# A four-layer conv/attention kernel on one core: TensorE steps of the later layers issued one or two turns after their other parts

## Chip, core and metric

The kernel runs on one core of a Trainium2 chip. The metric is the device time of one execution in microseconds (us): a median of several runs, beside the lowest and the highest. A profile is one more execution, taken by the hardware profiler. Four engines compute: TensorE (PE; its weight loads are shown apart as PEld), VectorE (DVE), ScalarE (ACT) and GpSimd (POOL). SyncE (SP) issues the DMAs. Each engine takes its own instructions in the order in which the program lists them, and waits where an operand or a buffer isn't ready.

## What is computed

Sixteen images of 128 channels and 28x28 pixels pass through four layers. Everything is fp32 (`_gn`, `_ln_t`: group and layer norm).

```python
# layer 0: minus the L1 distance of every 3x3 patch to 128 filters
x = x + _L0_conv_ref(_gn(x), L0_conv_W)       # -sum_k |w[f,k] - patch[k]|
# layer 1: two 3x3 convs, weights and activations quantized to 4 bits
x = _L1_conv_ref(x, w1, w2, ...)
t = _to_tokens(x)                             # 784 tokens of 128 channels
# layer 2: scores[i,j] = sum_d v[d]*tanh(Wi[j,d] + Wi[i,d]); softmax; values
t = t + _L2_attn_ref(_ln_t(t), W, v)
t = t + _L2_ffn_ref(_ln_t(t), ...)            # 8 experts, the best 2 mixed
# layer 3: causal linear attention, then 16 spectral filters as convolutions
t = t + _L3_attn_ref(_ln_t(t), W, b)
t = t + _L3_ffn_ref(_ln_t(t), sigma, phi, M_u, M_phi_plus, M_phi_minus, ...)
```

## The kernel before

**Layer 0 sets the beat.** The images go through in five groups (`GROUPS`) of 2, 4, 4, 4 and 2 images. |w - x| is made as ACT's Abs (L1444, "a" tiles) or, by 2 max(w, x) - w - x, as DVE's max (L1446) and add (L1448, "m" tiles): one wide instruction for one filter and one tap or two. `sums` (L1457) then adds over the channels on PE, with a one-column selector (`sel`) as weights, 32 output rows at a time, so four matmuls run side by side in the array. One round of this is a *tick*: one tile for each list of filters. The groups have 528, 960, 864, 864 and 416 ticks. `taps_of` makes the tiles of tick k+2 (`AHEAD = 2`) while `sums` uses those of tick k; the tiles lie in slots of the buffer `work`, five of them for groups of four images, of which other parts may borrow one or two (`lend`). The sums of a *phase* (a quarter or a half of a group's filters) gather in two PSUM banks; two pairs of banks (`acc0` to `acc3`) take turns from phase to phase, and `tap_sums_out` empties a pair with two ACT instructions (L607) three ticks after its phase.

**Everything else is laid into the ticks.** Four `Lane`s hold generators that yield `EV` (a step for the other engines) or `PE` (a step for TensorE): `plain` (small sums for layer 0), `convs` (layer 1), `chain` (layers 2 and 3 but for scores and filters, image after image) and `conv_out` (the spectral filters). In each tick `ahead` runs the due EV steps of every lane, `sums` follows, then `behind` runs the PE steps of the lanes in the same tick. A rate for each lane, times a pace for the group, says how many steps are due. The attention scores are a fifth stream: 196 turns for each image, each four rows of tanh on ACT (L1021) and four score products on PE (L1005) into one PSUM bank `sp`, issued in the same tick; `rows` gives them out. After 28 turns the bank is multiplied by `near` into `sc` (L1032, L1034) and started anew (L1001). A turn that may not run yet is lost.

The steps that are named below: the chain's attention values (`av`, L1089), expert products (`ex` L1174 on PE, then four multiply-adds on DVE, L1178) and linear attention (`nu`, L1227 and L1244) all pass through one PSUM bank `psx`. `spectral` takes 64 jobs for each image: three matmuls with a band matrix (`u`, L1336, 392, 264 and 136 columns) into the one bank `psu`, an ACT copy (L1346), and a matmul of the copy into `out` (L1339). Band and matrix come by DMA two jobs ahead.

After the last tick comes the tail (`stage["alone"]`): scores, chain and filters that are left. There a turn of scores makes its arguments with four DVE adds (L1014) and one wide ACT tanh (L1016), and the freed `acc` banks join `psx` and `psu`.

PE's order is fixed as it was written (`in_traced_order`); the order of the other engines is arranged by a scheduler when the program is built.

Of the kernel before, what the change touches and what calls it, by code (L numbers as in the profile page):

```python
# [53 lines left out]
class Group:  # L54
# [7 lines left out]
    def __init__(self, first, n, plan, rows, pace):  # L62
        self.first, self.n, self.plan, self.rows, self.pace = first, n, plan, rows, pace
        self.tall = n * HW
# [15 lines left out]
def tiles(taps):  # L80
# [16 lines left out]
GROUPS = (Group(0, 2, ALONE, 0.0, 1.0), Group(2, 4, EARLY, 0.85, 0.9), Group(6, 4, BESIDE, 1.95, 1.0),  # L97
          Group(10, 4, BESIDE, 1.95, 1.0), Group(14, 2, LATE, 3.2, 1.6))
# [25 lines left out]
STEP = 208  # L124
RATE_X, RATE_Y, RATE_C, RATE_A, RATE_0, RATE_T, RATE_Z = 1.2, 0.93, 1.5, 1.5, 0.9, 2.0, 0.75
# [5 lines left out]
class Lane:  # L131

    def __init__(self, rate=1.0):
        self.gens, self.turn = [], None
        self.holds, self.others = False, ()
        self.rate, self.due = rate, 0.0
# [4 lines left out]
    def run(self, turn):  # L143


        while self.gens:
            if self.turn is None:
                self.turn = next(self.gens[0], None)
                if self.turn is None:
                    self.gens.pop(0)  # L150
            elif self.turn != turn or (turn == PE and any(o.holds for o in self.others)):
                return False
            else:
                self.turn = next(self.gens[0], None)
                self.holds = turn == PE
                if self.turn is None:
                    self.gens.pop(0)
                return True
        return False

    def tick(self, pace):
        self.due += self.rate * pace
        n = int(self.due)
        self.due -= n
        return n
# [49 lines left out]
def kernel(ctx: ExitStack, tc: tile.TileContext, a: dict, out: bass.AP):  # L215
# [4 lines left out]
    three = ctx.enter_context(tc.tile_pool(name="three", bufs=3))  # L220
    scratch = ctx.enter_context(tc.tile_pool(name="scratch", bufs=1, space=bass.MemoryType.DRAM))
# [8 lines left out]
    turns = {"psx": 0, "psu": 0, "row": 0, "th": 0}  # L230

    def bank(pool, tag, more, name):
        turns[tag] = (turns[tag] + 1) % (1 + len(more)) if stage["alone"] else 0
        if turns[tag]:
            pool, tag = psacc, more[turns[tag] - 1]
        return pool.tile([P, 512], F32, tag=tag, name=name)

    def ps(name):
        return bank(psx, "psx", ("acc0", "acc1"), name)

    def small(name):
        return bank(psu, "psu", ("acc2", "acc3"), name)
# [175 lines left out]
    nc.vector.tensor_copy(edge[:NB], q[:NB, : 2 * P])  # L418
    taken, which_in = {}, []
    for plan in PLANS:  # L420
        taken[plan.name] = const.tile([2 * NB, P], F32, name=f"taken_{plan.name}")
        nc.vector.memset(taken[plan.name], 0.0)
# [9 lines left out]
        nc.vector.tensor_tensor(taken[plan.name][:NB], which[:NB, :P], which[:NB, P:], ALU.add)  # L432
# [122 lines left out]
    def plain_taps(g, phase, accs):  # L555
# [22 lines left out]
        seen = seen_in.ap[: 2 * NB].rearrange("p (h w) -> p h w", w=HW)  # L578
# [21 lines left out]
    def tap_sums_out(g, phase, accs):  # L600

        s = take(1)
        if s is None:
            return False
        t = s.ap[:, :T]
        for c in range(2):
            nc.scalar.activation(t[:, c * NCK : (c + 1) * NCK], accs[c][:, :NCK], AF.Identity,  # L607
                                 bias=sw[g.plan.name][:, phase : phase + 1])
# [3 lines left out]
        return True  # L612
# [160 lines left out]
    def spectral_weights():  # L773
# [56 lines left out]
        for j in range(NAR):  # L830
            yield EV
            m = three.tile([P, P], F32, tag="mat", name=f"m_ar{j}")
# [3 lines left out]
        for k in range(NK):  # L836
            yield EV
            me = three.tile([P, P], F32, tag="mat", name=f"m_even{k}")
            mo = three.tile([P, P], F32, tag="mat", name=f"m_odd{k}")
# [110 lines left out]

    state, scored, attended, spectral_in, spectral_out = {}, set(), set(), {}, set()

    def head(b):
# [17 lines left out]
        while b and b - 1 not in scored:  # L971
            yield EV
        wi = one.tile([P, T + SPAN], F32, tag="wi", name=f"wi{b}")
# [7 lines left out]
        state[b] = t, mv, rstd, wi  # L981

    products = []

    sp = pss.tile([P, 512], F32, name="sp")
    nc.vector.memset(sp, 0.0)

    def scores(b):
# [6 lines left out]
        def products_of(m, rows):  # L995
# [12 lines left out]
        for ib in range(NT):  # L1008
            for m in range(Q):
# [13 lines left out]
                products.append(lambda m=m, rows=rows: products_of(m, rows))  # L1023
                yield
            while products:
                products.pop(0)()
            while ib == 0 and b and b - 1 not in attended:
                yield
            lo = ib * TB
            n = min(SPAN, T - lo)  # L1030
            dst = sc[:, ib, :]
            nc.vector.tensor_tensor(cols(dst, lo, n), in_rows(sp[:, :n]), in_rows(near[:, :n]), ALU.mult)  # L1032
            if n < SPAN:
                nc.vector.tensor_tensor(cols(dst, 0, SPAN - n), in_rows(sp[:, n:SPAN]), in_rows(near[:, n:]), ALU.mult)  # L1034
        scored.add(b)
# [232 lines left out]
    def spectral(b):  # L1268
# [10 lines left out]
        def fetch(n):  # L1279
            if n < len(jobs):  # L1280
# [3 lines left out]
                m = three.tile([P, P], F32, tag="mat", name=f"mat{b}_{n}")  # L1284
# [3 lines left out]
        for to in range(2):  # L1288
# [38 lines left out]
            for n in [*mine, None]:  # L1327
                yield PE
                if n is not None:
                    _, k, odd = jobs[n]  # L1330
                    fetch(n + 2)
# [5 lines left out]
                while len(copied) > (stage["alone"] and n is not None):  # L1337
                    u, m0, lag = copied.pop(0)
                    nc.tensor.matmul(acc[:, lag:TH], m0, u[:, : TH - lag], start=False, stop=n is None and not copied)  # L1339
                if n is not None:  # L1340
                    yield EV
                    if stage["alone"]:
                        u = row(TH)
                    else:
                        u = two.tile([P, TH], F32, tag="u", name=f"us{b}_{n}")
                    nc.scalar.copy(u[:, :TH], q[:, :TH])  # L1346
                    copied.append((u, m, odd and (to ^ odd)))
# [12 lines left out]
    first = Lane(RATE_X)  # L1360
# [4 lines left out]
    plain, convs, chain, conv_out = Lane(), Lane(RATE_C), Lane(RATE_X), Lane(RATE_Y)  # L1365
    lanes = plain, convs, conv_out, chain
    for lane in (plain, convs, conv_out):
        lane.others = [x for x in (plain, convs, conv_out) if x is not lane]
    chain.add(quantized_weights(), token_constants(), spectral_weights(), head(0))
# [18 lines left out]
    pace = {"by": 1.0, "rows": 1.0}  # L1388

    def rows(rate):  # L1390
        due["units"] += rate * pace["rows"]
# [4 lines left out]
    def ahead():  # L1396


        chain.rate = RATE_A if "attending" in state else RATE_X if stage["group"] else RATE_0
        ns = [lane.tick(pace["by"]) for lane in lanes]  # L1400
        for n, lane in zip(ns, lanes):
            for _ in range(n):
                lane.run(EV)
        return ns

    def behind(ns):
        for n, lane in zip(ns, lanes):
            for _ in range(n if lane is convs else n > 0):
                lane.run(PE)

    def whole(rate):

        rows(rate)
        ns = ahead()
        while products:
            products.pop(0)()
        behind(ns)
# [48 lines left out]
    outs = []  # L1466
    parity = 0
    for k, (i, phase, _) in enumerate(seq):
# [4 lines left out]
        if new_group:  # L1473
            stage["group"] = i
            length = sum(x[0] == i for x in seq)
            end = k + length
            pace["rows"] = STEP * g.n / 2 / length
# [76 lines left out]
```

## Time and profile before

| what | us |
|---|---|
| three runs, median (lowest to highest) | 11791.2 (11789.41 to 11796.64) |
| the profiled execution, its own time | 11793.19 |
| its span, first to last instruction | 11791.4 |
| layer 0's groups in the trace, by the normed inputs (L548) | 47, 847, 2808, 5552, 8287 to 10058 |
| tail | 10058 to 11791 |
| last score product | 11466 |

The span is the time between the first and the last instruction of the core, and the time of the execution is the span and some two microseconds around it. A *busy* share is the union of an engine's instructions over the span. PE's ends are modelled: a matmul of 392 columns is drawn some 495 ns long, while the next one starts after 330 ns, so short idle times of PE don't show. "Idle before" and the waits are time in which an engine had nothing running, put down to the instruction that released it. PEclk is the share of full clock that TensorE was granted.

### The profile page before, as it was taken

How to read it: one execution, taken by the hardware profiler on the slowest of the kernel's cores; microseconds unless marked ns; L12 is line 12 of the kernel's file. 1: busy time of each engine (PE TensorE's matmuls, PEld its weight loads, DVE VectorE, ACT ScalarE, POOL GpSimd, SP SyncE). 2: the span in 40 equal slices, each digit the busy share in tenths (PEclk: the TensorE clock that was granted, in tenths of full speed). 3: DMA queues.
4: the chain of work that ended last, by engine and by line, in shares of the span. 5: the costliest groups of instructions: out<-in, count | busy, mean ns of one | idle time of the engine just before them, and what ended most of it. 6: DMA issues, size and time to landing. Idle time of an engine off the chain costs nothing.

```text
span 11791.4 us, 237615 instructions
## 1 busy us (share of the span) xinstructions
PE 11008.6 (93%) x99720; PEld 4985.0 (42%) x99720; DVE 10167.6 (86%) x12868; ACT 9795.4 (83%) x13475; POOL 185.9 (2%) x142
## 2 busy tenths in 40 slices
PE   7998888899989989899999999989999999999999
PEld 3443333344434434344344443434444444444446
DVE  9998999888888888888888889888888888988882
ACT  7887999788789798897878979788787888888882
POOL 1000000000000000000000000000000000000000
PEclk9999999999999999999999999999999999999999
DMA  1210000001001101011011110101111111121113
GB/s 33 63 38 5 4 1 4 5 21 46 25 11 30 34 21 37 24 35 47 24 29 36 34 36 20 38 18 38 39 36 41 45 34 41 46 58 52 56 54 109
DMA packets 435153, 402.95 MB, mean 34 GB/s; under 512 B 63429, under 2 KB 418045, under 8 KB 433709
## 3 DMA queue, kind: packets, MB, share of 16 engines
q1 hardware_dynamic: 433650, 385.96, 11.6%
q8 instruction: 786, 12.88, 0.4%
q14 instruction: 285, 2.33, 0.1%
q10 hardware_dynamic: 432, 1.77, 0.0%
HBM read 363.03 MB, written 24.49 MB: 33 GB/s over the span
## 4 chain that ended last, share of the span: by engine, by line
PE 64%; DVE 25%; ACT 7%; issue 3%; POOL 0%; DMA 0%; SPq 0%; DVEq 0%; ACTq 0%; POOLq 0%
PE acc L1457 26%; PE sp L1005 12%; PE u L1336 11%; DVE work L1446 10%; DVE work L1448 8%; PE out L1339 5%; ACT rows_in L1021 4%; DVE work L1014 3%; PE conv_ps L645 3%; ACT work L1444 2%; PE ex L1174 2%; PE av L1089 1%; DVE t L1178 1%; DVE rows_in L1446 0%; ACT work L1016 0%
## 5 line engine op out<-in xcount | busy, mean ns | idle before, releaser
L1021 ACT ACTIVATE rows_in<-wi 128x394 f32<-128x394 f32 x9576 | 5126.0, 618 | 538.8 <-PE sp L1005 535.1
L1446 DVE TENSOR_SCALAR work<-work,w 128x3024 f32<-128x3024 f32 (+5 forms) x3050 | 4444.7, 1484 | 841.4 <-PE acc L1457 797.6
L1457 PE MATMUL acc<-work,sel_m 128*32 128x392 f32 (+3 forms) x39248 | 3905.2, 495 | 254.2 <-DVE work L1448 197.5
L1444 ACT ACTIVATE work<-work,w 128x2916 f32<-128x2916 f32 (+2 forms) x1242 | 2872.9, 2331 | 633.8 <-PE acc L1457 578.7
L1448 DVE SCALAR_TENSOR_TENSOR work<-work,w 128x2916 f32<-128x2916 f32 (+3 forms) x1154 | 3202.2, 2780 | 11.0
L1457 PEld LDWEIGHTS acc<-work,sel_m 128*32 128x32 f32 x39248 | 1257.2, 111 | 2223.7 <-issue 1677.0
L1005 PE MATMUL sp<-rows_in,vz 128*32 128x394 f32 x19152 | 2171.7, 499 | 13.5 <-ACT rows_in L1021 13.2
L1457 PE MATMUL acc<-work,sel_a 128*32 128x351 f32 (+2 forms) x16592 | 1742.4, 480 | 29.3 <-ACT work L1444 29.2
L1336 PE MATMUL u<-band,up 128*128 128x392 f32 (+2 forms) x6144 | 1629.9, 402 | 8.5 <-ACT y L650 3.9
L1336 PEld LDWEIGHTS u<-band,up 128*128 128x128 f32 x6144 | 1095.1, 190 | 953.4 <-issue 264.4
L1016 ACT ACTIVATE work<-work 128x1576 f32<-128x1576 f32 x742 | 1089.2, 1522 | 112.1 <-DVE work L1014 107.7
L1005 PEld LDWEIGHTS sp<-rows_in,vz 128*32 128x32 f32 x19152 | 700.2, 111 | 980.8 <-issue 655.2
L1014 DVE TENSOR_SCALAR work<-wi 128x394 f32<-128x394 f32 x2968 | 1039.1, 420 | 6.2 <-PE sp L1005 3.2
L1457 PEld LDWEIGHTS acc<-work,sel_a 128*32 128x32 f32 x16592 | 593.5, 111 | 773.2 <-issue 667.9
L1005 PE MATMUL sp<-work,vz 128*32 128x394 f32 x5936 | 591.7, 508 | 70.2 <-ACT work L1016 69.8
L1339 PE MATMUL out<-us,mat 128*128 128x392 f32 (+1 forms) x1366 | 563.0, 494 | 0.0
L1346 ACT COPY us<-u 128x392 f32<-128x392 f32 x683 | 322.1, 472 | 211.9 <-PE u L1336 211.0
L1178 DVE SCALAR_TENSOR_TENSOR t<-ex,gate,t 128x128 f32<-128x128 f32 x896 | 310.6, 348 | 141.9 <-PE ex L1174 129.2
L1346 ACT COPY rows_in<-u 128x392 f32<-128x392 f32 x341 | 164.5, 482 | 303.3 <-PE u L1336 302.0
L1174 PE MATMUL ex<-ew,xt 128*128 128x512 f32 x448 | 251.5, 645 | 106.0 <-DVE t L1178 96.2
L1005 PEld LDWEIGHTS sp<-work,vz 128*32 128x32 f32 x5936 | 148.8, 110 | 387.6 <-ACT work L1016 196.3
L1339 PE MATMUL out<-rows_in,mat 128*128 128x392 f32 (+1 forms) x682 | 280.1, 495 | 0.0
(319 smaller groups left out, 5707.0 us busy)
## 6 DMA issues: line engine op xcount, KB each, us to landing
band<-band SPq DMA_DIRECT2D x1024, 196.0 KB
mat<-mats SPq DMA_DIRECT2D x1024, 64.0 KB
lags<-lag_mats SPq DMA_DIRECT2D x80, 192.0 KB
work<-q_L_conv_w SPq DMA_DIRECT2D x16, 576.0 KB
ew<-in_L_ffn_expert_w_dram SPq DMA_DIRECT2D x16, 512.0 KB
work<-in_x_dram SPq DMA_DIRECT2D x10, 784.0 KB
eb<-eb_rows SPq DMA_DIRECT2D x16, 448.0 KB
band<-band_out SPq DMA_DIRECT2D x32, 196.0 KB
```

Source lines behind the costliest of these rows:

```text
L1005: nc.tensor.matmul(sp[32 * j : 32 * j + 32, lo : lo + WIN], vz[:, 32 - m : 64 - m], rows[j], start=m == 0, stop=m == Q - 1, skip_group_che ...
L1014: nc.vector.tensor_scalar(th[:, j, :], wi[:, i + Q * j : i + Q * j + WIN], wi[:, i + Q * j : i + Q * j + 1], None, ALU.add)
L1016: nc.scalar.activation(th, th, AF.Tanh)
L1021: nc.scalar.activation(rows[j], wi[:, i + Q * j : i + Q * j + WIN], AF.Tanh, bias=wi[:, i + Q * j : i + Q * j + 1])
L1174: nc.tensor.matmul(q, blk(xt, i), ew[:, 4 * h : 4 * h + 4, :], start=True, stop=True)
L1336: nc.tensor.matmul(q[:, P * i : TH], up[:, to ^ odd, i, :], t[:, :w], start=i == 0, stop=i == 2)
L1339: nc.tensor.matmul(acc[:, lag:TH], m0, u[:, : TH - lag], start=False, stop=n is None and not copied)
L1346: nc.scalar.copy(u[:, :TH], q[:, :TH])
L1444: nc.scalar.activation(part, x, AF.Abs, bias=wk, scale=-1.0)
L1446: nc.vector.tensor_scalar(part, x, wk, None, ALU.max)
L1448: nc.vector.scalar_tensor_tensor(part, x, wk, part, ALU.max, ALU.add)
L1457: nc.tensor.matmul(in_rows(accs[c][32 * j : 32 * j + 32, :NCK])[:, lo - 14 * c : hi - 14 * c, c0:c1], sel[kind][:, 31 - m : 63 - m], d.rea ...
```

## The change

The lanes get a rate for each group in steps a tick, and a lag: after a lane's EV step its next PE step may run only that many ticks later. In groups two to four the lags are 1 (plain, convs), 2 (conv_out) and 1 (chain); in the last group only conv_out has one, of 1; the first group and the tail have none. In each tick a lane runs at most one PE step. `hurry` drops the lag for the step that makes `wi`.

```diff
-GROUPS = (Group(0, 2, ALONE, 0.0, 1.0), Group(2, 4, EARLY, 0.85, 0.9), Group(6, 4, BESIDE, 1.95, 1.0),
-          Group(10, 4, BESIDE, 1.95, 1.0), Group(14, 2, LATE, 3.2, 1.6))
+BALANCED = (0.5, 0.75, 0.27, 0.75), (1, 1, 2, 1)
+GROUPS = (Group(0, 2, ALONE, 0.0, (0.4, 0.6, 0.35, 0.355), (0, 0, 0, 0)),
+          Group(2, 4, EARLY, 0.4, (0.5, 0.75, 0.25, 0.5), (1, 1, 2, 1)),
+          Group(6, 4, BESIDE, 0.94, *BALANCED), Group(10, 4, BESIDE, 0.94, *BALANCED),
+          Group(14, 2, LATE, 1.6, (0.8, 0.8, 0.4, 1.0), (0, 0, 1, 0)))
...
+RATE_T, LAST_RATES = 2.0, (1.0, 1.0, 0.4, 1.5)
...
+            elif turn == PE and self.ready > Lane.ticks:
+                return False
             else:
                 self.turn = next(self.gens[0], None)
                 self.holds = turn == PE
+                if turn == EV:
+                    self.ready = Lane.ticks + (0 if self.hurry else self.lag)
...
+    def steps(self):
+        self.due = min(self.due + self.rate, 2.0)
+        n = 0
+        while self.due >= 1.0 and self.run(EV):
+            self.due -= 1.0
+            n += 1
         return n
```

The eight PSUM banks are dealt out anew: layer 0's sums have two banks instead of four, so `tap_sums_out` empties them at the end of the phase's last tick, one half on ACT and one on DVE, and the next phase's first tick puts the score products ahead of its `sums`. The scores get two banks, and the filters' `u` gets two.

```diff
     def ps(name):
-        return bank(psx, "psx", ("acc0", "acc1"), name)
+        return bank("psx", [(psx, "psx"), (psacc, "acc0")][: 1 + stage["alone"]], name)
     def small(name):
-        return bank(psu, "psu", ("acc2", "acc3"), name)
+        return bank("psu", [(psu, "psu0"), (psu, "psu1"), (psacc, "acc1")][: 2 + stage["alone"]], name)
...
-        for c in range(2):
-            nc.scalar.activation(t[:, c * NCK : (c + 1) * NCK], accs[c][:, :NCK], AF.Identity,
-                                 bias=sw[g.plan.name][:, phase : phase + 1])
+        by = sw[g.plan.name][:, phase : phase + 1]
+        nc.scalar.activation(t[:, :NCK], accs[0][:, :NCK], AF.Identity, bias=by)
+        nc.vector.tensor_scalar(t[:, NCK:], accs[1][:, :NCK], by, None, ALU.add)
```

With two banks the scores of the next 28 turns may begin while the last bank is being emptied; a new function `settle`, called at the head of `ahead`, empties a bank one or two ticks after its last turn, and not before the image ahead has been attended.

```diff
-    sp = pss.tile([P, 512], F32, name="sp")
-    nc.vector.memset(sp, 0.0)
+    sps = [pss.tile([P, 512], F32, tag=f"sp{i}", name=f"sp{i}") for i in range(2)]
...
+    def settle():
+        while blocks:
+            b, ib, sp, ready = blocks[0]
+            if ready > Lane.ticks or (ib == 0 and b and b - 1 not in attended):
+                return
+            blocks.pop(0)
...
+            nc.vector.tensor_tensor(cols(dst, lo, n), in_rows(sp[:, :n]), in_rows(near[:, :n]), ALU.mult)
```

The spectral filters go two at a time: one PE step first adds the two copies of the step before into `out`, then makes `u` for two jobs; one EV step copies both. In the tail, before, the matmul of a copy followed one job later; now it opens the next step.

```diff
-            for n in [*mine, None]:
+            for n0 in [*mine[::2], None]:
                 yield PE
-                if n is not None:
+                for u, m0, lag in copied:
+                    nc.tensor.matmul(acc[:, lag:TH], m0, u[:, : TH - lag], start=False,
+                                     stop=n0 is None and u is copied[-1][0])
...
+                for n in (n0, n0 + 1):
...
                     for i in range(3):
                         w = TH - P * i
                         nc.tensor.matmul(q[:, P * i : TH], up[:, to ^ odd, i, :], t[:, :w], start=i == 0, stop=i == 2)
...
+                yield EV
+                for at, (q, m, lag) in enumerate(copied):
+                    u = two.tile([P, TH], F32, tag="u", name=f"us{b}_{n0 + at}")
+                    nc.scalar.copy(u, q[:, :TH])
```

Smaller parts: the per-plan selectors `taken` share one tile, placed by one more DMA each at the start; the `mat` buffers are four instead of three; the next image's `wi` waits until the last score turn of the image before has been issued, not until its bank has been emptied.

## Prediction

> **What bounds the kernel now.** The page comes first: three engines are nearly equally loaded, and none is full.
>
> ```profile
> span 11791.4 us, 237615 instructions
> PE 11008.6 (93%) x99720; PEld 4985.0 (42%) x99720; DVE 10167.6 (86%) x12868; ACT 9795.4 (83%) x13475; POOL 185.9 (2%) x142
> ```
>
> Next the busy times by stage, groups two to five and the tail (columns: length; busy and count of PE, PEld, DVE, ACT, POOL; granted PE clock; DMA share; GB/s).
>
> ```profile
> 847.00:2808.00 1961.00, 1741.43 (x18821) 711.51 (x18815) 1738.24 (x1151) 1721.68 (x1754) 15.91 (x8) 0.96 0.04 10
> 2808.00:5552.00 2744.00, 2565.88 (x23310) 1112.00 (x23304) 2376.51 (x2122) 2287.10 (x3554) 35.60 (x19) 0.97 0.10 29
> 5552.00:8287.00 2735.00, 2584.95 (x23616) 1137.96 (x23610) 2369.81 (x2098) 2310.68 (x3600) 40.52 (x20) 0.98 0.11 32
> 8287.00:10058.00 1771.00, 1740.34 (x14602) 838.43 (x14598) 1529.83 (x2101) 1481.57 (x2789) 25.97 (x15) 1.00 0.14 40
> 10058.00:11791.40 1733.40, 1625.50 (x10659) 843.98 (x10651) 1356.33 (x4296) 1283.20 (x1251) 29.13 (x22) 0.98 0.22 62
> ```
>
> PE is the fullest engine in every stage but the second group, where DVE and ACT are as full. Where PE is 98% busy (8287 to 10058) its clock is 1.00; where it idles the clock falls to 0.96 to 0.98. So a wait of PE costs twice: itself, and slower matmuls around it. DMA is far from a bound. The question is what PE waits for in groups two to four, where the lags will be. The waits of PE alone from 847 to 8287:
>
> ```profile
> PE acc L1457 <- DVE work L1448: 180.3, 112, 7.1
> PE ex L1174 <- DVE t L1178: 88.7, 32, 7.6
> PE nu L1227 <- DVE t L1244: 49.7, 19, 5.3
> PE acc L1457 <- DVE work L1446: 46.5, 9, 10.7
> PE gt L1157 <- DVE gate L1154: 24.4, 3, 8.4
> PE av L1089 <- DVE t L1098: 22.0, 11, 3.3
> PE mb L1074 <- DVE dg L1069: 15.7, 4, 6.8
> PE sp L1005 <- ACT rows_in L1021: 13.2, 17, 1.9
> PE sp L1001 <- DVE sc L1034: 13.0, 10, 2.6
> ```
>
> By target, the view's 37 rows add up to 235 us for layer 0's tiles (`acc`), 27 for the scores (`sp`) and 284 for the lanes, 546 in all. The lanes' 284 is what a lag can reach: ex 93, nu 54, gt 24, mb 22, av 22, mir 12, the rest 57. Last, prices:
>
> ```profile
> 3903.81 2.70 PE L1457 MATMUL acc<-work,sel_m 128*32 128x378 f32 x32
> 3906.44 1.60 PE L1336 MATMUL u<-band,up 128*128 128x392 f32 x6
> 3907.88 0.82 PE L1339 MATMUL out<-us,mat 128*128 128x392 f32 x2
> ...
> L1016 ACT ACTIVATE work<-work 128x1576 f32<-128x1576 f32 x742 | 1089.2, 1522 | 112.1 <-DVE work L1014 107.7
> L1005 PE MATMUL sp<-work,vz 128*32 128x394 f32 x5936 | 591.7, 508 | 70.2 <-ACT work L1016 69.8
> ```
>
> Side by side, four 32-column matmuls cost one slot of 0.33 us (32 records in 2.70). One filter costs PE 1.44 us in `u` and 0.66 in `out` (the modelled end, 0.16, taken off).
>
> **The change part by part.** Both programs have the same 50,590 matmuls, so PE's own work (some 10,000 us at these pitches) neither grows nor shrinks. What can change is waiting, clock, and which work lies together.
>
> *Lags (groups two to four).* The lists of both built programs, in groups three and four, tell how far apart two uses of the chain's bank stand. A tick there is 2744/864 = 3.2 us. PE to PE goes from 0.80 to 1.76 ticks for av, 1.15 to 1.8 for the mirrors, 1.36 to 1.65 for ex, 1.30 to 1.48 for nu; a filter's copy goes from 2.2 to 3.4 ticks ahead of its matmul. Against the mean wait: ex gains 0.29 tick = 0.9 us of 2.8 (88.7/32), a third, 31 us; nu 0.6 of 2.6, a quarter, 12 us; av and mirrors 3 us against 2, nine tenths, 31 us; gt one tick of 8.1, 10 us; mb 0.8 of 22, 17 us; half of the rest's 57, 28 us. Together -129 us (bounds 0 and -284). The last group and the tail have no lag for the chain: nothing there.
>
> *Clock.* Not granted from 847 to 8287: 0.04 x 1961 + 0.03 x 2744 + 0.02 x 2735 = 215 us. If it goes with the waits, 129/546 of it comes back: -51 (bounds 0 and -112, that is 284/546).
>
> Here a rule of the skill speaks against the change. The rows: the tail already cycles PE through three banks each for `ps` and `small`, and is granted 0.98, no less than the single-bank groups before. The Trainium skill, "TensorE: Matmul & The Clock Gate", section "A second HAM failure mode: psum-queue depth-cycling", says that cycling through PSUM banks each iteration leaves micro-idle times that make the clock fall and recover again and again. Were the clock to fall by 0.01 over 847 to 10058 for it, the sum would be 92 us higher; I go by the rows.
>
> *Two score banks.* PE's waits for the emptied bank (L1001) are 13.6 us before 8287 and 13.0 after it, by the same view of each part; -20 (bounds -27 and 0; the cover, a second bank, is emptied one or two ticks after its last turn).
>
> *Work moved.* 155 turns of scores leave the tail (742 to 587 there), since turns are no longer lost. PE: at 0.84 ns a column, 1591, 2312, 2352, 1573 and 1479 us of matmuls stand in groups two to five and the tail before, and 1682, 2324, 2438, 1596 and 1267 after: 212 us move forward. The four groups take 9211/7828 = 1.177 us per us of PE work and the tail 1733/1479 = 1.172: +1. ACT pays 155 x 4 x 0.535 (5126.0/9576) = 332 us more in the groups and 155 x 1.47 less in the tail; DVE 155 x 1.40 less there. PE waits 69.8/742 for each tail turn, 155 fewer: -15 (bounds -15 and 0). That ACT can take 332 us is due to its idle 16% in the groups; without that cover see the second rival.
>
> *Two banks for tap sums.* The next phase's `sums` must wait until ACT and DVE have emptied the banks (0.57 us, L607), both behind what they run at that moment: up to one 3.25 us multiply-add, and on PE's side up to four tanh (2.1 us) for products now standing ahead of `sums`. Cover: PE's rest of the old tick (lanes and products, 3.2 - 1.3 us) and 0.66 of the next products, 2.5 us. So 0 to 3.4 us for each of 15 boundaries; I take 1.5: +23 (bounds 0 and +51). DVE's queue holds the next tile behind this wait, but tiles for two ticks are already made. ACT loses 16 x 0.57, DVE gains it: nothing.
>
> *Filters in pairs.* PE works 4.2 us on end instead of 2.1, in 360 turns from 847 to 10058. Meanwhile DVE and ACT can make tiles ahead until the slots are full: five slots, three in use, two ticks, 6.3 us, so the burst is hidden. While `convs` has borrowed a slot (some 40 ticks for each of two image pairs in 864, 9%) it isn't: 33 turns x 1 us = +33 (bounds 0 and 360 x 2.1 = 756). In the tail the copy has no turn between any more; the first `out` (0.66) covers the second copy (0.48, L1346): nothing, and up to 152 x 0.48 = 73 without that cover. SP's loads (196 + 64 KB a filter) are issued in the same order and at the same distance, two jobs: nothing, with DMA at 0.22 of its share.
>
> Sum: -129 - 51 - 20 + 1 - 15 + 23 + 33 = -158 on the span's 11791.4: 11633; with the 1.8 us around the span and a median 2 us under the profiled time, **11633** for the median.
>
> **Rivals.**
> 1. *Much more comes back.* The lags take all 284 us of the lanes and 112 of clock, and, because PE is no longer late, half of layer 0's 235: -284 - 112 - 118 - 20 - 15 + 56 = -493, 11300. For it: DVE itself waits for PE's slots (L1446, 797.6 us), so an early PE feeds the others. Against: ex and nu, half of the lane waits, gain only 0.2 to 0.3 tick.
> 2. *It doesn't do what it says.* The scheduler orders DVE and ACT anew, and ex and nu hardly move apart; waits pass to ACT, which has 332 us more: if the groups keep ACT's share of 7802/9211 = 85%, they grow by 332/0.847 = 392 us while the tail loses 155 x 1733/742 = 362. With the other terms left out: 11820 less 30 for clock, 11790, no change. Against: ACT is not the fullest engine.
> 3. *Slower: bursts empty the pipeline.* If PE's 4.2 us bursts stop DVE and ACT by more than they can make ahead, each of 360 turns costs up to 2.1 us. Without its own 33 the sum is -191, so from 0.53 us a turn on it decides; at 0.75 it is +270 - 191 = +79, 11870. For it: ACT waits for PE's slots 578.7 us and for score rows 535.1 already. Against: the two free slots.
>
> **How the numbers follow.** Forecast (11500 to 11760): 0.52. First rival 0.12, second 0.10, third 0.26. A change of 0.2% (24 us) is about what this kernel's measurement can tell from none. Faster: 0.52 + 0.12 and a little of the second, 0.65; same 0.09; slower 0.26. The range 11410 to 11870 takes in the forecast's own, part of the first rival (lanes and clock in full, without layer 0's half), no change, and the third at 0.75 us a turn. Left out are deeper gains and bursts that are hardly covered.
>
> **What would show it.** Right: in groups two to four PE's waits for ex, nu, av and mirrors fall to about half and the granted clock rises by 0.005 or so; L1001's waits nearly vanish; the tail becomes some 1733 x 1267/1479 = 1485 us, the groups together 9211 + 250 - 145 = 9316. Wrong: PE's idle time before `acc` grows by more than the lanes' shrinks (the third rival: with DVE and ACT waiting for `acc` far beyond 797.6 and 578.7), ACT's busy share in the groups above 90% with PE waiting for L1021's rows (the second), or `sums` waiting 3 us and more at each phase's start for the emptied banks.

## The result, and the profile after

The changed kernel takes 11858.0 us (median of four runs, 11851.65 to 11863.49); the kernel before takes 11792.9 beside it (11789.41 to 11796.64). The ratio is 1.0055, with an interval of 1.0038 to 1.0072: slower by 66 us, where 158 us less were forecast.

The first lines of its page:

```profile
span 11857.3 us, 236865 instructions
PE 11053.8 (93%) x99720; PEld 5178.5 (44%) x99720; DVE 9971.7 (84%) x12262; ACT 9898.6 (83%) x13924; POOL 214.6 (2%) x142
```

TensorE's records are the same in number, and no engine's share has moved by more than some two points. PE has nothing running for 783 us before and 804 after; the other 45 us of the 66 lie in its busy time, where a lower clock (0.975 for 0.977) and idle times too short to show can't be told apart. The stages, groups two to five and the tail (columns as before: length; busy and count of PE, PEld, DVE, ACT, POOL; granted PE clock; DMA share; GB/s):

```profile
845.50:2914.80 2069.30, 1888.90 (x19449) 851.41 (x19445) 1745.66 (x1158) 1817.34 (x1950) 22.47 (x8) 0.96 0.05 14
2914.80:5709.80 2795.00, 2565.36 (x23686) 1139.98 (x23690) 2396.29 (x2205) 2393.15 (x3745) 53.07 (x21) 0.97 0.10 27
5709.80:8562.40 2852.60, 2674.50 (x24156) 1218.88 (x24152) 2401.65 (x2204) 2410.98 (x3788) 47.99 (x21) 0.98 0.12 32
8562.40:10376.00 1813.60, 1784.19 (x14845) 887.95 (x14841) 1525.49 (x2079) 1526.41 (x2879) 29.00 (x16) 1.00 0.14 40
10376.00:11857.30 1481.30, 1390.90 (x8882) 747.14 (x8874) 1106.98 (x3514) 1039.45 (x1042) 23.17 (x18) 0.98 0.24 65
```

The tail has become 1481 us, 4 less than the forecast's 1485. The four groups take 9531 us where 9316 were forecast. Part of their growth is work from the tail: at each group's own ratio of time to PE work before, the moved matmuls alone give 2073, 2758, 2835 and 1797 us. Groups three, four and five lie 37, 18 and 17 us above that; group two 4 below. (Not all of the moved turns of scores are turns no longer lost, as the forecast had it: group two's rate for them also rose, from 0.85 x 416/960 = 0.37 to 0.40 a tick, and 42 of the 155 were gained there, partly by that.) The 180 us that the lags should have taken out of groups two to four are not to be seen.

What PE waits for in groups two to four (target and line, what released it and its line; us in all, times, the longest):

```profile
PE ex L1208 <- DVE t L1212: 138.9, 42, 7.3
PE acc L1492 <- DVE work L1483: 126.3, 89, 3.9
PE nu L1261 <- DVE t L1278: 68.2, 33, 4.1
PE tc_n L952 <- DVE n L934: 64.2, 15, 8.8
PE gt L1191 <- DVE gate L1188: 39.8, 6, 10.8
...
PE sp L1042 <- ACT rows_in L1062: 12.5, 17, 1.0
...
PE av L1123 <- DVE t L1132: 1.5, 2, 1.0
```

The rows are the ones shown before, at new line numbers (L1174 is L1208, L1227 is L1261, L1457 is L1492). `av` fell from 22.0 to 1.5, and the waits for an emptied score bank are gone from the view. But `ex` rose from 88.7 to 138.9, `nu` from 49.7 to 68.2, `gt` from 24.4 to 39.8, and `tc_n` (L936 before, not among the rows shown of it) from 2.5 to 64.2. Summed by target over the whole view, the lanes' waits are 376 us, up from 285; those for layer 0's tiles fell from 235 to 198.

DVE waits longer for PE too. From the same view of the whole run, all engines:

```profile
DVE work L1481 <- PE acc L1492: 1011.3, 615, 9.6
ACT rows_in L1062 <- PE sp L1042: 564.7, 371, 9.6
ACT work L1479 <- PE acc L1492: 437.8, 292, 10.6
PE ex L1208 <- DVE t L1212: 150.3, 50, 7.3
PE acc L1492 <- DVE work L1483: 143.3, 108, 3.9
```

DVE waits 1011 us for slots that PE frees (797.6 before), while PE waits longer for DVE's steps in the lanes: each is late at some times, not one of them always. ACT waits less, 438 us for slots and 565 for score rows where it was 579 and 535.

### The profile page after: what moved, and what is told of

Read it like the earlier page. It is cut to its first block, busy times and chain, and to the rows that moved or that the text cites. A ratio compares the mean times of both kernels' runs of the same rounds, so it can differ in the third digit from the quotient of the medians.

```text
span 11857.3 us, 236865 instructions
## 1 busy us (share of the span) xinstructions
PE 11053.8 (93%) x99720; PEld 5178.5 (44%) x99720; DVE 9971.7 (84%) x12262; ACT 9898.6 (83%) x13924; POOL 214.6 (2%) x142
## 4 chain that ended last, share of the span: by engine, by line
PE 63%; DVE 22%; ACT 9%; issue 4%; POOL 1%; DMA 1%; SPq 0%; DVEq 0%; ACTq 0%; POOLq 0%
PE acc L1492 24%; PE sp L1042 12%; PE u L1375 11%; DVE work L1481 9%; DVE work L1483 7%; PE out L1364 6%; ACT rows_in L1062 5%; ACT work L1479 3%; PE conv_ps L661 3%; PE av L1123 2%; PE ex L1208 2%; DVE work L1055 1%; DVE t L1212 1%; ACT work L1057 1%; PE out L1333 1%
## 5 line engine op out<-in xcount | busy, mean ns | idle before, releaser
L1062 ACT ACTIVATE rows_in<-wi 128x394 f32<-128x394 f32 x10196 | 5440.0, 616 | 570.2 <-PE sp L1042 564.7
L1492 PE MATMUL acc<-work,sel_m 128*32 128x378 f32 (+3 forms) x39176 | 3950.8, 495 | 174.6 <-DVE work L1483 143.3
L1479 ACT ACTIVATE work<-work,w 128x2916 f32<-128x2916 f32 (+2 forms) x1250 | 2885.7, 2325 | 475.6 <-PE acc L1492 437.8
L1042 PE MATMUL sp<-rows_in,vz 128*32 128x394 f32 x20392 | 2431.5, 500 | 12.9 <-ACT rows_in L1062 12.7
L1492 PEld LDWEIGHTS acc<-work,sel_m 128*32 128x32 f32 x39176 | 1334.9, 111 | 1984.4 <-issue 1490.7
L1492 PE MATMUL acc<-work,sel_a 128*32 128x378 f32 (+3 forms) x16656 | 1794.2, 485 | 66.9 <-ACT work L1479 49.5
L1375 PE MATMUL u<-band,up 128*128 128x392 f32 (+2 forms) x6144 | 1460.1, 387 | 0.9 <-DMA band<-band 0.9
L1492 PEld LDWEIGHTS acc<-work,sel_a 128*32 128x32 f32 x16656 | 617.1, 112 | 792.5 <-issue 595.7
L1057 ACT ACTIVATE work<-work 128x1576 f32<-128x1576 f32 x587 | 861.2, 1530 | 112.5 <-DVE work L1055 111.6
L1055 DVE TENSOR_SCALAR work<-wi 128x394 f32<-128x394 f32 x2348 | 822.5, 425 | 8.4 <-PE sp L1042 7.6
L1364 PE MATMUL out<-us,mat 128*128 128x392 f32 (+1 forms) x2048 | 815.3, 518 | 0.3 <-ACT us L1381 0.3
L1364 PEld LDWEIGHTS out<-us,mat 128*128 128x128 f32 x2048 | 344.8, 189 | 447.7 <-issue 234.6
L1212 DVE SCALAR_TENSOR_TENSOR t<-ex,gate,t 128x128 f32<-128x128 f32 x896 | 311.0, 348 | 130.5 <-PE ex L1208 117.4
L1208 PE MATMUL ex<-ew,xt 128*128 128x512 f32 x448 | 263.4, 673 | 150.5 <-DVE t L1212 150.3
L1123 PEld LDWEIGHTS av<-vx,sc 128*128 128x128 f32 x1568 | 184.4, 191 | 47.0 <-issue 31.9
```

The source lines that it names most:

```text
L1042: nc.tensor.matmul(sp[32 * j : 32 * j + 32, lo : lo + WIN], vz[:, 32 - m : 64 - m], rows[j], start=m == 0, stop=m == Q - 1, skip_group_che ...
L1055: nc.vector.tensor_scalar(th[:, j, :], wi[:, i + Q * j : i + Q * j + WIN], wi[:, i + Q * j : i + Q * j + 1], None, ALU.add)
L1057: nc.scalar.activation(th, th, AF.Tanh)
L1062: nc.scalar.activation(rows[j], wi[:, i + Q * j : i + Q * j + WIN], AF.Tanh, bias=wi[:, i + Q * j : i + Q * j + 1])
L1208: nc.tensor.matmul(q, blk(xt, i), ew[:, 4 * h : 4 * h + 4, :], start=True, stop=True)
L1375: nc.tensor.matmul(q[:, P * i : TH], up[:, to ^ odd, i, :], t[:, :w], start=i == 0, stop=i == 2)
```

## The experiments

Four explanations were open: the lags don't work; the pairs of filters cost more than was thought; the scheduler puts the DVE steps behind too many tiles; the lanes' new rates bunch the work. "Lane waits" below is PE's idle time in groups two to four before anything but `acc` and `sp`, summed as above: 285 us before, 376 after. Each ratio is to runs of the kernel before in the same session on the chip, with medians of 11788.0 to 11792.9 us.

### What the lags are worth

`e1`: the changed kernel with every lag at 0.

```diff
-BALANCED = (0.5, 0.75, 0.27, 0.75), (1, 1, 2, 1)
+BALANCED = (0.5, 0.75, 0.27, 0.75), (0, 0, 0, 0)
...
-          Group(2, 4, EARLY, 0.4, (0.5, 0.75, 0.25, 0.5), (1, 1, 2, 1)),
+          Group(2, 4, EARLY, 0.4, (0.5, 0.75, 0.25, 0.5), (0, 0, 0, 0)),
...
-          Group(14, 2, LATE, 1.6, (0.8, 0.8, 0.4, 1.0), (0, 0, 1, 0)))
+          Group(14, 2, LATE, 1.6, (0.8, 0.8, 0.4, 1.0), (0, 0, 0, 0)))
```

> The changed kernel with every lag set to 0, all else kept (rates, pairs of filters, banks). Theory L (the lag itself is what costs: PE waits for the chain rose from 284 to 376 us in groups two to four because a lagged bank is held longer): the lane waits go back to about 284 us and the time to 11770, within 30 of the kernel before. Theory B (the bursts of paired filters and the shared tap banks cost, and the lag takes a little off): slower than the changed kernel, 11880 to 11950. If the lag does nothing either way: 11858 within 24.

12065.0 us, 1.0235 (1.022 to 1.0251). The lags take 207 us away, and lane waits go from 509 without them to 376 with them. That is further up than any of the three expectations had it. So the lags do bring time; something else in the change costs more than they bring.

### The order of DVE

The scheduler may put a tile of layer 0 between two steps of a lane. In the changed kernel the four multiply-adds of one expert (L1212), 0.35 us each, are drawn out so (DVE, then PE; start, length, engine, line, operation, tiles, count, and the wait in brackets):

```profile
6928.08 0.35 DVE L1212 SCALAR_TENSOR_TENSOR t<-ex,gate,t 128x128 f32<-128x128 f32 x1
6928.34 1.85 DVE L1481 TENSOR_SCALAR work<-work,w 128x3136 f32<-128x3136 f32 x1
6930.10 0.35 DVE L1212 SCALAR_TENSOR_TENSOR t<-ex,gate,t 128x128 f32<-128x128 f32 x1
6930.36 3.37 DVE L1483 SCALAR_TENSOR_TENSOR work<-work,w 128x3024 f32<-128x3024 f32 x1
6933.63 0.35 DVE L1212 SCALAR_TENSOR_TENSOR t<-ex,gate,t 128x128 f32<-128x128 f32 x1
...
6934.13 2.05 PE L1208 MATMUL ex<-ew,xt 128*128 128x512 f32 x2 [5.56 <-DVE t L1212]
```

Two tiles of 1.85 and 3.37 us lie between three steps that need 1.05 us together, and PE stands idle 5.56 us. Counted over the traces of groups two to four, 0.87 tiles lie inside each group of four; before, it was 0.83. `e2` ties DVE to the written order, `e3` ACT as well, `e4` does to the kernel before what `e2` does to the changed one, and `e8` ties DVE in groups two to four alone.

```diff
-    in_traced_order(tc, (mybir.EngineType.PE,))
+    in_traced_order(tc, (mybir.EngineType.PE, mybir.EngineType.DVE))
```

```diff
+            marks[i] = len(tc.nc.cur_bb.bb.instructions)
...
     in_traced_order(tc, (mybir.EngineType.PE,))
+    in_traced_order(tc, (mybir.EngineType.DVE,), marks[1], marks[4])
```

> The changed kernel with VectorE's order fixed as written, as TensorE's is. In the trace of the changed kernel the four multiply-adds that free the chain's bank stand one by one between layer 0's tiles (0.87 tiles inside each such group of four), so that PE waits up to 5.6 us for them. Theory S (the order that the scheduler gives VectorE undoes the lag): PE's wait for ex falls from 138.9 us in groups two to four to under 60, the lane waits in all from 376 to under 200, and the time to 11600 to 11750. Theory B: ex falls too, but the time stays above 11820, since VectorE and ScalarE go on waiting for free slots.

> The same with ScalarE's order fixed as written too. Theory S: as with VectorE's order alone or up to 60 us better, since copies then stand ahead of the next tile. Against it: a fixed order of ScalarE lets a copy that waits for PE hold up the tanh rows behind it; then slower than with VectorE's alone by 20 to 150 us.

> The kernel before with VectorE's order fixed as written. Theory S says that this order, not the lag, decides: PE's wait for ex (88.7 us in groups two to four) falls under 60 and the time by 50 to 150 us, to 11640 to 11740. If the written order only helps where there is a lag (PE then meets a step that VectorE has finished): no gain, 11790 to 11900, for in the kernel before the PE step follows its VectorE part in the same tick.

> The changed kernel with VectorE's order fixed as written only in groups two to four; in the run with the order fixed everywhere those stages took 2013, 2778 and 2848 us for 2069, 2795 and 2852, while the start (+53), the first group and the tail (+251) lost. If the stages are independent: 11858 - 77 = 11780, level with the kernel before or a little faster. If the written order only puts off waits to the tail: 11850 or more.

| run | us | ratio (interval) |
|---|---|---|
| `e2`, DVE written | 12122.9 | 1.0285 (1.0268 to 1.0302) |
| `e3`, DVE and ACT written | 12365.3 | 1.049 (1.0474 to 1.0505) |
| `e4`, before, DVE written | 12080.2 | 1.0248 (1.0233 to 1.0263) |
| `e8`, DVE written in groups two to four | 11783.6 | 0.9994 (0.9985 to 1.0004) |

Everywhere, the written order loses, and in both kernels much the same (+265 us in the changed one, +292 in the one before); `e2` lies where theory B had it, above 11820, and `e3` and `e4` are slower than any forecast for them. By stages the loss is in the set-up and the first group (77 us, 74 with the kernel before) and in the tail (251 and 295 us). Groups two to four are shorter in both: by 78 us in `e2`, and by 119 in `e4` (1913, 2686 and 2722 us for 1961, 2744 and 2735). Kept to these groups it gains 74 us, near the 77 that were expected, and the waits of the whole run of `e8` say where:

```profile
DVE work L1481 <- PE acc L1492: 567.4, 330, 9.3
...
PE acc L1492 <- DVE work L1483: 269.4, 166, 5.6
...
PE ex L1208 <- DVE t L1212: 74.5, 49, 3.6
```

`ex` is halved (150.3 to 74.5) and DVE waits 567 us for slots instead of 1011; in exchange PE waits longer for DVE's tiles (143.3 to 269.4). So the scheduler's order is a real cost in these groups, but one that the kernel before pays as well, and more of it (119 us in `e4`, with 0.83 tiles in a group of four): it can't account for the step from one kernel to the other.

### The lanes' rates

The new rates are higher than what the old paces gave. In steps a tick, in groups three and four, old and new are 0.48 and 0.5 (plain), 0.72 and 0.75 (convs), 0.448 and 0.54 (filters, counted singly), 0.6 and 0.75 (chain; the 0.6 stands for 0.58 in general and 0.72 while an image's attention runs). `e5` brings the old ones back in the changed kernel, lags and all else kept; `e10` those of the filters alone, `e13` those of the chain alone.

```diff
-BALANCED = (0.5, 0.75, 0.27, 0.75), (1, 1, 2, 1)
+BALANCED = (0.48, 0.72, 0.224, 0.6), (1, 1, 2, 1)
...
-          Group(2, 4, EARLY, 0.4, (0.5, 0.75, 0.25, 0.5), (1, 1, 2, 1)),
+          Group(2, 4, EARLY, 0.4, (0.39, 0.59, 0.18, 0.47), (1, 1, 2, 1)),
```

> The changed kernel with the lanes' rates of groups two to four set to what the kernel before gives them (filters 0.224 pairs a tick for 0.27, chain 0.6 for 0.75; in the second group 0.18 and 0.47), lags and all else kept. Counted from the built programs, PE's work in 32 ticks of groups three and four spreads by 10.0 us about its mean of 86.3 before the change, by 15.9 about 88.2 after it, and by 12.4 about 87.7 here: filters go faster and then pause. Theory R (the faster rates bunch PE's work, which then swings between too much and too little): 100 to 170 us faster than the changed kernel, 11690 to 11760, groups three and four together about 120 us shorter. If rates don't matter: 11858 within 24, perhaps a longer tail.

> The changed kernel with only the filters' rate put back (0.224 pairs a tick, 0.18 in the second group); the chain stays at 0.75 and 0.5. PE's work in 32 ticks of groups three and four then spreads by 13.1 us (15.9 in the changed kernel, 12.4 with all rates put back). Theory R, by that spread: four fifths of the gain of 120 us, 11760 +- 30. If it is the chain's rate that costs: 11830 to 11858.

> The changed kernel with only the chain's rate put back (0.6, 0.47 in the second group); filters stay at 0.27 and 0.25 pairs. The filters' rate alone gave 41 us of the 120. If the two add: 79 us, 11780 +- 25. If what counts is how evenly PE's whole work lies (32 ticks of groups three and four spread by 15.5 us here, hardly less than 15.9): 11830 to 11858, and then the two rates only help together.

`e5` takes 11738.6 us, 0.9957 (0.9942 to 0.9972): faster than the kernel before, and 119 us faster than the changed one, by nothing but how fast the lanes are asked to run in groups two to four. Groups three and four shrink from 2795 and 2853 to 2734 and 2791 us, as forecast. With the filters' rate alone (`e10`) it is 11816.6, 1.0027 (1.0017 to 1.0038): 41 us, where the spread of PE's work had let 100 be expected. With the chain's alone (`e13`) it is 11856.6, 1.0056 (1.004 to 1.0073): nothing. By stages, with PE's waits in groups two to four, in us:

| kernel | groups two to four | group five | tail | lane waits | waits for `acc` |
|---|---|---|---|---|---|
| after | 7717 | 1814 | 1481 | 376 | 198 |
| `e10`, filters' old rate | 7678 | 1811 | 1477 | 346 | 196 |
| `e13`, chain's old rate | 7685 | 1852 | 1474 | 276 | 255 |
| `e5`, all old | 7557 | 1851 | 1483 | 243 | 217 |

The chain's old rate makes groups two to four 32 us shorter and leaves work to group five, which grows by 38; so it brings nothing in all. `e5` pays the same 38 there, and gains 160 before it, where `e10` and `e13` together gain 71: the rates don't add up one by one. Nor is it enough to look at the lanes' waits: `e13` takes 100 us off them, but PE then waits 57 us longer for tiles.

What the rates do to the work is seen in a stretch in which one image's filters run, and in the pause after it until the next one's begin; columns as in the stages. Before:

```profile
4372.00:4883.00 511.00, 486.14 (x4274) 218.11 (x4274) 427.75 (x374) 412.00 (x646) 3.49 (x3) 0.98 0.13 36
4883.00:5085.00 202.00, 180.64 (x1835) 74.45 (x1834) 184.99 (x170) 187.64 (x293) 4.38 (x2) 0.96 0.06 15
```

After:

```profile
4324.00:4751.00 427.00, 416.53 (x3619) 202.90 (x3616) 337.32 (x295) 357.88 (x568) 1.88 (x2) 0.98 0.16 43
4751.00:5009.00 258.00, 222.22 (x2247) 89.77 (x2246) 238.42 (x232) 231.44 (x365) 11.65 (x3) 0.94 0.04 10
```

With the old rates (`e5`):

```profile
4321.00:4816.00 495.00, 475.58 (x4195) 225.09 (x4196) 409.08 (x369) 420.56 (x665) 4.77 (x3) 0.98 0.14 37
4816.00:5002.00 186.00, 168.87 (x1744) 68.75 (x1744) 174.01 (x163) 178.25 (x279) 4.37 (x2) 0.97 0.06 17
```

After, the filters are done in 427 us instead of 511, with PE 98% busy and DVE at 79%; then comes a pause of 258 us instead of 202, with PE 86% busy and DVE 92%. In `e5` PE is 96% and 91% busy, DVE 83% and 94%. The image ahead of this one gives 502 and 214 us before, 416 and 267 after, 491 and 182 in `e5`; there the pauses are alike in PE's share (86, 86 and 88%) and differ in length.

Bunching as the way in which the rates cost is argued from this, not shown: a stretch that PE bounds and one that DVE and ACT bound can hardly lend each other their idle time, since tiles are made two ticks ahead and the stretches last eighty ticks and more (258 us at 3.2). Both images together take 1368 us after and 1354 in `e5` with the same work (PE busy 1279 and 1278 us). These 7 us an image make some 56 us over the eight images whose filters run in groups two to four, an estimate that covers about half of the 119.

The same can be counted in the programs: the PE work (0.84 ns a column) of each 32 ticks in groups three and four has a mean of 86 to 88 us in all these kernels, but a standard deviation of 10.0 before, 15.9 after, 15.5 in `e13`, 13.1 in `e10` and 12.4 in `e5`. That orders the four lagged kernels as their times do, 11858, 11857, 11817 and 11739, but it doesn't size them: 2.8 us of spread go with 41 us between after and `e10`, and 0.7 us with 78 between `e10` and `e5`.

### Filters in pairs

`e6` has one filter a turn in the changed kernel, with the old loop (rate 0.5, lag 1; 0.8 without lag in group five and the tail). `e9` has the old rates and no lags, with pairs; `e14` the same with single filters.

```diff
-BALANCED = (0.5, 0.75, 0.27, 0.75), (1, 1, 2, 1)
+BALANCED = (0.5, 0.75, 0.5, 0.75), (1, 1, 1, 1)
...
-            for n0 in [*mine[::2], None]:
+            for n in [*mine, None]:
```

> The changed kernel with one filter a turn again (the loop of the kernel before, rate 0.5 a tick with a lag of 1 in groups two to four, 0.8 after), all else kept. Theory B (bursts of two filters stop VectorE and ScalarE, which wait 1011 and 438 us for PE's acc): 60 to 200 us faster than the changed kernel, 11660 to 11800, with VectorE's wait for acc back near 850. If the pair is harmless or saves switching: 11860 to 11920.

> The changed kernel with the old rates of the run before this one and every lag at 0. Theory R with lags as a gain of their own: the lags were worth 207 us at the faster rates (12065 to 11858); at the old rates chain and filters ask less often for their banks, so 120 to 200 us: 11860 to 11940. If the lags only mended what the faster rates broke: at most 40 us, 11740 to 11780.

> Old rates, every lag 0, one filter a turn: what is left of the change is the banks, one PE step a lane and tick, and 155 turns fewer in the tail. With pairs this was 11843, 53 us above the kernel before. If the pair is what is left: 11790 +- 25, level with the kernel before. If the pair is not: 11830 or more.

| run | us | ratio (interval) | lane waits |
|---|---|---|---|
| `e6`, single | 11804.0 | 1.0012 (1.0003 to 1.0022) | 325 |
| `e9`, old rates, no lags, pairs | 11842.6 | 1.0047 (1.0032 to 1.0062) | 357 |
| `e14`, the same, single | 11770.9 | 0.9986 (0.9977 to 0.9995) | 307 |

Pairs cost 72 us without lags (`e9` less `e14`). With lags at the new rates `e6` is 54 us faster than the changed kernel, but its filters also go a little slower (0.5 a tick for 0.54 in groups three and four; all the way to 0.448 was worth 41 us in `e10`) and have a lag of 1 for 2, so not all of the 54 need be the pair's. By stages, in us, one filter a turn instead of two changes:

| from, to | groups two to four | group five | tail |
|---|---|---|---|
| after, `e6` | -21 | -4 | -27 |
| `e9`, `e14` | -9 | -36 | -26 |
| `e11`, `e12` (below) | +36 | -26 | -28 |

Only the tail's share is the same each time. In groups two to four, where the bursts were feared, the pairs cost at most 21 us. DVE's wait for `acc` goes only from 1011 to 981 us in `e6`, where about 850 were expected, and from 953 to 897 between `e9` and `e14`. `e9` itself lies between its two expectations; `e14` is where it was expected if the pair is what costs.

### Two banks for the tap sums

`e7` is the kernel before with the changed kernel's two banks in place of four: emptied at once, the products ahead of the next phase's `sums`, both halves still on ACT.

```diff
-            parity = 1 - parity
-            accs = [psacc.tile([P, 512], F32, tag=f"acc{2 * parity + c}", name=f"acc{i}_{phase}_{c}") for c in range(2)]
+            accs = [psacc.tile([P, 512], F32, tag=f"acc{c}", name=f"acc{i}_{phase}_{c}") for c in range(2)]
...
+        if first and k:
+            while products:
+                products.pop(0)()
...
-            outs.append((k + 3, g, phase, accs))
+            assert tap_sums_out(g, phase, accs)
```

> The kernel before with two banks for tap sums: emptied at the end of the phase's last tick (both halves on ScalarE), next phase's products ahead of its sums, nothing else changed. My sum had +23 us for it (0 to 51): 11790 to 11840. If shared banks are what costs: 11900 or more, with PE waiting for L607 at each of 15 phase starts.

11762.1 us, 0.9978 (0.9968 to 0.9987): 26 us faster by its ratio, where the forecast had 23 slower. PE waits 15.6 us in the whole run for ACT's emptying (L607).

### What the findings make together

`e11` is the changed kernel with the old rates (`e5`) and DVE written in groups two to four (`e8`); `e12` is `e11` with single filters (0.448 a tick, lag 1).

```diff
-BALANCED = (0.5, 0.75, 0.27, 0.75), (1, 1, 2, 1)
+BALANCED = (0.48, 0.72, 0.448, 0.6), (1, 1, 1, 1)
...
+    in_traced_order(tc, (mybir.EngineType.DVE,), marks[1], marks[4])
```

> Old rates, lags, and VectorE's order as written in groups two to four. If the two gains (120 and 75 us) add: 11665 +- 30, 1% faster than the kernel before. If both take the same waits: 11710 to 11740.

> The same with one filter a turn (0.448 a tick, lag 1; 0.36 in the second group; 0.8 after). If the pair's cost of 54 us is its own: 11610 +- 40. If the pair cost only because PE's work was bunched at the faster rate, which the old rates mend: 11650 to 11700.

`e11` takes 11649.7 us, 0.9884 (0.9869 to 0.9898), and `e12` 11627.0, 0.9866 (0.9849 to 0.9882): 231 us less than the changed kernel and 161 less than the one before (11788.0 beside it). The gains of the old rates and of the written order add (89 us of the second on top of `e5`); single filters bring 23 more, not 54, and not in groups two to four. The first lines of `e12`'s page, and the waits for `nu` and `ex` in its groups two to four:

```profile
span 11623.7 us, 237577 instructions
PE 11025.9 (95%) x99720; PEld 5086.9 (44%) x99720; DVE 10049.6 (86%) x12262; ACT 9894.4 (85%) x13924; POOL 220.0 (2%) x142
```

```profile
PE nu L1261 <- DVE t L1278: 14.8, 20, 1.3
PE ex L1208 <- DVE t L1212: 13.9, 10, 3.7
```

With lags, old rates and a written order together, `ex` is 13.9 us where it was 88.7 before and 138.9 after; lane waits are 83 us in all, as in `e11`.

## Why the prediction was wrong

One path of single steps leads from the kernel before to the changed one:

| step | from, to | forecast | measured |
|---|---|---|---|
| banks, `settle`, the new counting of steps, turns that leave the tail, their work in the groups | before (11788), `e14` (11771) | -20 - 15 + 23 + 1 = -11 | -17 |
| filters in pairs | `e14`, `e9` (11843) | +33 | +72 |
| lags, with their clock | `e9`, `e5` (11739) | -129 - 51 = -180 | -104 |
| lanes' rates | `e5`, after (11858) | no term of their own | +119 |

So of the distance between 158 us faster and 66 slower, the rates make 119, the lags 76 and the pairs 39. In another order the steps have other sizes: at the new rates the lags take 207 us, and without lags the rates cost 222 (`e1` less `e9`). Each is the size of a step beside these neighbours, and the intervals make it good to some 20 us.

**The step that failed** is "*Work moved*". It priced the work that goes from the tail into the groups at "1.177 us per us of PE work" there and 1.172 in the tail, "+1", and between stages the tail came out at 1481 us for 1485 (with 27 of them due to the pairs: it is 1453 in `e6` and `e14`). But the new rates also move work inside a group, from one tick to another, and that was left at nothing: no term of the sum stands for it. Where +1 stood, the faster rates cost 119 us (`e5` to after) and lift lane waits by 133; without them the change is faster than the kernel before (`e5`), on the side that was forecast, though by 50 us and not by 158. That the rates cost is shown by `e5`; that they cost by bunching the work is the reading that fits best. A price for each microsecond of PE work then holds only where the mixture of work stays the same.

The first row of the table fits by luck in part. The banks for tap sums alone gave -26 where it has +23 (`e7`), so the rest of the row, forecast at -34, came to about +9.

**The lags** were sized well in the sum of the waits: 129 us were forecast for the lanes, and they fall by 133 at the new rates (`e1` to after) and by 114 at the old (`e9` to `e5`). The rows behind the sum are another matter. `ex`, forecast at -31, falls by 82 at the new rates (221 to 139) and not at all at the old ones (112 to 113). "PE's waits for ex, nu, av and mirrors fall to about half" came true for `av` and the mirrors (34 us before, 5 after), but not for `ex` and `nu`, which even at the old rates (`e5`) are 113 and 53 us for 93 and 54 before. In time the lags brought 207 and 104 us around the forecast's 180. The granted clock goes the same way as the lanes' waits, 0.969 in `e1` and 0.975 after, 0.975 in `e9` and 0.979 in `e5`, with `e13` as an exception (276 us of lane waits, 0.976).

**Filters in pairs** were mis-sized: 33 forecast, 72 measured without lags, at most 54 in the changed kernel, and 23 between `e12` and `e11`, with a written order. The 33 stood for groups two to five; in the tail the pairs were put at nothing, with 73 at most, and cost 26 to 28 us in each of the three comparisons. The third rival's bursts, which decide from 0.53 us a turn on (191 us), are far from that: groups two to five together give 25, 45 and -10. Its sign in the trace, DVE waiting for `acc` beyond 797.6 us, came out at 1011, but the rates raise that wait more (`e5` has 887) than the pairs do (`e6` has 981); ACT's, 437.8 for 578.7, went the other way. So this sign alone would have pointed to the wrong part.

**The banks for tap sums** had the wrong sign, -26 for +23. The wait that was feared is small: in groups two to four of the changed kernel PE waits 7.9 us for ACT's emptying and 4.2 for DVE's. Why two banks gain is open. **Two score banks** did what they should in the trace (L1001's 13.6 us are gone); their own share of the time was not run apart, since it needs the banks that the tap sums give up.

**The second rival** named the scheduler, and it does cost: 74 us (`e8`) and 89 at the old rates (`e11` less `e5`). But the kernel before has it too (119 us in `e4`), and no wait passed to ACT as it said: ACT is 86% busy in groups two to four, and PE's waits for its score rows are 12.5 us for 13.2. **The first rival**'s 514 us of lags, clock and layer 0's tiles were not seen; the lags brought 104 to 207.

For the clock, groups two to five and the tail are granted 0.96, 0.97, 0.98, 1.00 and 0.98, the same as before, though scores and `u` now take turns between two banks each. The rule that the forecast set aside (the Trainium skill, "TensorE: Matmul & The Clock Gate", section "A second HAM failure mode: psum-queue depth-cycling") tells of a kernel in which cycling through PSUM banks made the clock go up and down again and again. This case's rows show no such fall.

**A reading** of the prediction's price rows is off without effect on the sum. Their counts are records, of which a matmul here has two (`u` has six for the three matmuls of one filter). So 0.33 us is the slot of four records side by side, and four matmuls take two such slots.

What stays open: by which mechanism the rates cost, and whether the chain's rate or those of `plain` and `convs` make the 78 us between `e10` and `e5`; the spread over 32 ticks changes little there (13.1 to 12.4). Rates below the old ones, which would say whether 0.448 is itself too fast, were not tried.

## What to carry to other kernels

Where several streams are laid into one beat and two engines are nearly full, a stream's rate is a cost of its own, here 119 us for the same work. One that runs fast and then pauses makes stretches in which one engine is full and stretches in which another is, so look at the work of each engine over short windows as well as over stages, and try the rates one by one and together. A gain that a trace doesn't show may be there and be paid out again: undo the parts one at a time, and in both settings of the other parts. Where a scheduler puts long independent instructions between short dependent ones, try a fixed order stage by stage: here it gained in the three loaded groups and lost in the set-up, the first group and the tail.

## What was not expected of the hardware

In the pauses between filters the granted clock fell to 0.94 and 0.95 with PE 86% busy, while in the stretches with filters, at 95 to 98% busy, it was 0.98 and 0.99. That holds before the change (0.94 and 0.96 in its two pauses) as after it (0.95 and 0.94), so the bunching doesn't show in the depth of the fall, and the mean over the run hardly moves (0.977 before, 0.975 after). Where the lanes' waits go, it does move: the two kernels with the fewest, 83 us, are granted 0.985 (`e11`) and 0.984 (`e12`), and `e12` runs the same 99,720 records of matmuls in 11025.9 us of busy time instead of 11053.8.
